# Handing work across the loop boundary of a planned four-layer kernel: the last tail, the first scan operands, the first depthwise operands and a sample's load

## The chip, the cores and the metric

The kernel runs on one core of one Trainium2 chip. The core has five engines, each with its own in-order queue: TensorE (PE), VectorE (DVE), ScalarE (ACT), GpSimd (POOL) and SyncE (SP), which only issues transfers here. The metric is the device time of the whole program in microseconds (us), the median of several runs; lower is better.

## The reference

The input is x of shape (64, 96, 28, 28) in float32. Four layers follow each other, each with a residual.

```python
# layer 0, per sample: a conditional inverted bottleneck, 576 hidden channels, 4 experts
rw  = softmax(relu(mean(x) @ r_w1.T + r_b1) @ r_w2.T + r_b2)      # routing weights
h   = silu(bn1(conv1x1(x, exp_w)))
h   = silu(bn2(dwconv5x5(h, sum_e rw[e] * dw_w[e])))              # per-sample kernels
h   = h * sigmoid(silu(mean(h) @ se_w1.T) @ se_w2.T)              # squeeze and excite
x   = x + bn3(conv1x1(h, sum_e rw[e] * pw_w[e]))
# layers 1 and 3: inverted bottleneck with fixed weights
h   = relu(bn1(conv1x1(x, w1)))
h   = relu(bn2(dwconv3x3(h, wd)))
x   = x + bn3(conv1x1(h, w3))
# layer 2: each sample is cut into four 14 x 14 images; for each image
n   = group_norm(x);  a = silu(conv1x1(n, p1));  u = silu(dwconv3x3(conv1x1(n, p2)))
# selective scan in 4 directions (rows, columns, both reversed), 196 steps, 16 states
h_t = exp(delta_t * A) * h_(t-1) + (delta_t * u_t) * B_t;   y_t = <h_t, C_t> + D * u_t
y   = a * group_norm(sum of the 4 directions)
x   = x + y * sigmoid(relu(mean(y) @ ca_w1.T) @ ca_w2.T)
```

## The kernel before

**Stages.** Samples run through the four layers as a pipeline. `slot` (L1462) issues the work of one step. In the slot of sample t, layer 2 works on sample t (`mamba`, in two halves of two images), layer 1 on t+1, layer 0 on t+2 and layer 3 on t-1; the first expansion of layer 1 for sample t+2 is issued too ("ahead"). At the slot's end the finished sample t-1 is stored (L1477) and sample t+3 is loaded (L1487). Four tiles `xt` hold the samples in flight.

**Blocks.** A block is a stretch of slots that is planned as one. There are nine executions of three blocks: the opening with slot 0, a hardware loop (`For_i`, L1543) with eight slots in its body, run seven times (56 slots), and a last block of seven slots. A plan knows nothing of the block before it or after it; at the jump back to the loop's start all engines meet.

**The planner.** `Plan.op` records an operation with its engine, an estimated cost, what it reads and writes, and a due time. `Plan.run` then places the operations one by one: on each engine those that can start within a grace of each other compete, and the earliest due goes first. The order that results is written down as the order of each engine's queue. The due time is a nominal one, slot number times `T` (144.0) plus a place within the slot, plus a shift from the table `DUE`, which has an entry for each kind of operation (a kind is the function that issues it and the layer it is for). An operation is not started more than 45 us ahead of its due time. Where `run` expects TensorE to idle, it fills the hole with matmuls of zeros (L527).

**Buffers.** Every pool in `POOLS` has a fixed number of buffers, and `run` picks one when it places the operation that first writes it: 3 of `rep` and `wd`, 2 of `B` and `C`, 4 of `dd`, 1 of `y`, 5 PSUM banks `ps`. `take` makes a new tile under the buffer's name.

**Layer 2.** `head` computes the norms, u, a and the scan's inputs, and sends them to DRAM (`bcd`, `ddd`). `scans` (L1254) fetches them spread over lanes with SyncE: B, three dd tiles and C (L1251). ScalarE computes the decays (L1322), VectorE the products b (L1340), then a forward scan h (L1345) and a backward scan g (L1350), 12 pairs for each half; GpSimd adds and multiplies (L1300); TensorE sums over states into y (L1274). `tail` (L1368) takes y, starting with L1377 on VectorE, and does the group norm (L1096 to L1116), the gating (L1407), two small matmuls and the gate (L1429), which writes the sample's half.

**Convolutions.** `expand` issues the 1x1 matmuls (L717, L747), their evictions (L701) and the stores to DRAM `ex` (L734, L760). `load` fetches for a unit of channels the shifted rows `rep` (L772) and the weights `wd` (L801 from DRAM; for layer 0 POOL builds them, L576). `depthwise` runs on TensorE (L819), with evictions on ScalarE (L830). `project` is L888 on TensorE, and L900 adds the residual on VectorE. Layer 0 also has `routing` (L927 to L956, mixing at L916 and L918).

Of the kernel before, what the change touches and what calls it, by code (L numbers as in the profile page):

```python
# [163 lines left out]
def pack_l2(ins):  # L164
# [54 lines left out]
    -11, 24, -20, -15, -10, 25, -7, -25, 9, 6, 16, -2, 2, 11, -18, 5, 31, -17, -8, -16, 22, 1, -6, 26, 19, -9,  # L219
    11, 14, -14, 13, -11, 0, -18, 13, -4, -1, 16, -5, 22, -5, 12, -9, -6, 2, 3, 1, 4, 28, 1, 25, -4, -5, 9,  # L220
    -17, -3, -4, 21, -13, -6, 9, 17, 21, -20, 30, 3, 7, -13, 3, -11, 11, 40, 2, -12, 24, -9, -21, 29, -7, 15,
    14, 13, -10, 9, -1, 8, 4, 15, 8, 24, -22, -9, 11, -21, -8, -4, 16, 4, -12, 7, 8, -17, 33, -3, -13, 8, 24,
    -3, 10, 22, 24, 12,)


class Buf:


    def __init__(self, pool):
        self.pool, self.ap, self.users, self.left, self.end = pool, None, 0, 0, 0.0  # L230
# [9 lines left out]
class Plan:  # L240
# [15 lines left out]
    def __init__(self, kernel):  # L256
        self.k = kernel
        self.ops = []
        self.writer, self.readers, self.latest = {}, {}, {}
        self.due, self.tag = 0.0, None  # L260

    def buf(self, pool):
        return Buf(pool)
# [46 lines left out]
    def run(self, start=0.0):  # L310
        free = dict.fromkeys(GRACE_KEYS, start)
        slots = {name: [None] * n for name, n in self.k.slots.items()}
        queue = {e: [] for e in free}
# [7 lines left out]
        def place(o):  # L321

            t = 0.0
            need = {}
            for b in o.allocs:
                need[b.pool] = need.get(b.pool, 0) + 1
            for pool, n in need.items():
                ends = sorted(0.0 if s is None else s.end for s in slots[pool] if s is None or not s.left)
                if len(ends) < n:
                    return None  # L330
                t = max(t, ends[n - 1])
            return t

        while left:
# [55 lines left out]
            for b in o.allocs:  # L390
                s = slots[b.pool]
                i = min((i for i in range(len(s)) if s[i] is None or not s[i].left), key=lambda i: s[i].end if s[i] else 0.0)
                s[i] = b
                b.ap = self.k.take(b.pool, i)
# [9 lines left out]
            self.emit(o, last)  # L404
        self.span = max(free.values())
# [54 lines left out]
class Kernel:  # L460
    T = 144.0
# [26 lines left out]
    def __init__(self, ctx, tc, x, out, blobs, packs):  # L488
# [12 lines left out]
        for i in range(4):  # L501
            nc.sync.dma_start(self.xt[i], self.x[i])
# [14 lines left out]

        self.b = pool("terms", 1, space=PSUM).tile([P, 1024], F32, name="b")
# [12 lines left out]
    def take(self, pool, i):  # L531
        return self.pools[pool].tile(self.POOLS[pool][1], F32, tag=f"{pool}{i}", name=pool)
# [50 lines left out]
    def setup(self, fold, banks):  # L583
# [91 lines left out]
        self.npad = self.ndecay = 0  # L675

# [99 lines left out]
    def load(self, d, u):  # L776

        nc, pl, k, cb, layer = self.nc, self.plan, d["k"], d["cb"], d["layer"]
        pl.tag = layer
        if layer == 0:  # L780
            ch, n = 64 * u, 4
        else:
            ch, n = P * u, 4 if u < 4 else 2
        rep, wd = pl.buf("rep"), pl.buf("wd")
        pl.op(
            SP, 0.32 * (k + 1), lambda: self.rows(d, rep, ch, n),
            r=[("ex", d["exkey"], ch // P)], w=[rep], nbytes=(k + 1) * cb * n * 1792, land=4.2 if n == 4 and k == 3 else 2.8,
        )
        m = n * k * 2
        lanes = (k + 1) * cb  # L790

        def spread():
            self.spread_taps(
                wd()[:lanes, : m * cb].rearrange("k (n c) -> k n c", c=cb), d["kern"]()[:, 40 * u : 40 * u + 40], d["c"]("mask")
            )

        if layer == 0:
            pl.op(POOL, 1.45, spread, r=[d["kern"]], w=[wd])
        else:
            pl.op(  # L800
                SP, 0.55, lambda: nc.sync.dma_start(wd()[:, : m * cb], self.taps[layer][u][:, : m * cb]),  # L801
                w=[wd], nbytes=P * m * cb * 4,
            )
        d.setdefault("units", {})[u] = rep, wd
# [236 lines left out]
    def convs(self, base, span, jobs, first=None, ahead=None):  # L1041
# [12 lines left out]
        for i, (d, after) in enumerate(jobs):  # L1054
# [6 lines left out]
            for u in range(units):  # L1061
                pl.due = at(u / units) - 14.0
                self.load(d, u)
# [184 lines left out]
    def spread(self, pool, key, due, src):  # L1248
        nc, pl = self.nc, self.plan
        t = pl.buf(pool)  # L1250
        pl.op(SP, 0.58, lambda: nc.sync.dma_start(t(), src), r=[key], w=[t], nbytes=602112 if pool == "dd" else 401408, due=due)  # L1251
        return t

    def scans(self, q, at):  # L1254
# [3 lines left out]
        y = q["y"] = pl.buf("y")  # L1258

        def states(lane, k):  # L1260

            v = self.bcd[i2][lane + 8 * k : lane + 8 * k + 8].rearrange("(a n u) l -> a n (u l)", a=1, u=2)
            return v.to_broadcast([32, 4, 2 * HALF])

        def channels(j):

            v = self.ddd[i2][32 * j : 32 * j + 32].rearrange("c (a l) -> c a l", a=1)
            return v.to_broadcast([32, 4, 3 * HALF])
# [37 lines left out]
        for k in range(2):  # L1306
            B = self.spread("B", ("bcd", i2), at(6 * k) - 14.0, states(0, k))
            if k == 0:
                for j in range(J):
                    dd[j] = self.spread("dd", ("ddd", i2), at(2 * j) - 14.0, channels(j))  # L1310
            Cs = self.spread("C", ("bcd", i2), at(6 * k) - 10.0, states(32, k))
            ys = []
            for j in range(J):
                i = 2 * (J * k + j)
                n = self.ndecay % len(self.decays)
                self.ndecay += 1
                fs = self.decays[n]

                def decay(fs=fs, d=dd[j], k=k, j=j):
                    for u in range(2):  # L1320
                        at = (2 * k + u) * J + j
                        nc.scalar.activation(  # L1322
                            fs[:, :, u, :, :SEQ],
                            d()[:, :2].rearrange("p o (i l) -> p o i l", i=2),
                            AF.Exp,
                            scale=self.A[:, at : at + 1],
                        )

                pl.op(ACT, 1.9, decay, r=[dd[j]], w=[("decay", n)], table=EXP, due=at(i) - 9.0)
# [112 lines left out]
    def mamba(self, t, base, span, more):  # L1442
# [6 lines left out]
        for h, q in enumerate(qs):  # L1449
            self.scans(q, lambda i: at(h * n + i))  # L1450
# [8 lines left out]
            self.tail(q)  # L1459
        yield  # L1460

    def slot(self, i, t, load, store, expanded=True, last=0, lead=0.0):  # L1462
# [5 lines left out]
        m = self.mamba(t, base - lead, span, last < 2)  # L1468
        next(m)
        jobs = []  # L1470
        if last < 2:
            jobs.append((self.job(1, t + 1, 0), None))
# [12 lines left out]
        if load is not None:  # L1485
            pl.due = base + span - 10.0
            pl.op(SP, 0.4, lambda: nc.sync.dma_start(self.xt[(t + 3) % 4], load), w=keys(t + 3), nbytes=301056)  # L1487
        for _ in m:
            pass

# [44 lines left out]
def mk_conv_seq_kernel(ctx, tc, x, out, blobs, packs):  # L1535
# [5 lines left out]
    k.slot(0, 0, None, None, lead=45.0)  # L1541
    pl.run(-150.0)
    with tc.For_i(0, (n - 4) // 8, 1) as it:  # L1543
        pl = k.block()
        for j in range(8):
            k.slot(j, 1 + j, at(k.x, it * 8 + 4 + j), at(k.out, it * 8 + j))
# [3 lines left out]
    for j in range(left):  # L1550
        load = k.x[n - left + 3 + j] if j < left - 3 else None
        k.slot(
            j, 1 + j, load, k.out[n - left - 1 + j], expanded=j < left - 1, last=max(0, j + 3 - left)
# [25 lines left out]
```

## Time and profile before

| what | value |
|---|---|
| median of 3 runs | 10218.62 us (10200.85 to 10236.85) |
| the profiled execution: time | 10215.28 us |
| the profiled execution: span, first to last instruction | 10213.4 us |
| granted TensorE clock, mean | 0.960 of full speed |
| transfers | 2262 MB, 222 GB/s |
| forward and backward scans | 2751.2 and 2726.3 us of VectorE |

The profile is of one execution. "Busy" is the time in which an engine carries out instructions; a wait is put down to what ended last before it was over. Rows of the timeline give start and length in us, engine, line of the kernel, operation, and tiles as out<-in with partitions and elements; a bracket at the end is the idle time before the instruction and what released it. SPq and ACTq are the queues of SyncE and ScalarE as they issue transfers.

### The profile page before, as it was taken

The numbers are of one execution on the slowest core, as the hardware profiler recorded it, in microseconds if no ns is written. First come the engines' busy times: TensorE is split into PE (matmuls) and PEld (weight loads), VectorE is DVE, ScalarE is ACT, GpSimd is POOL, SyncE is SP. The second block draws the span as 40 slices with busy tenths as digits, with TensorE's granted clock in tenths as the row PEclk, the third lists the DMA queues.
The fourth block names the chain that finished last, engine by engine and source line by source line (L and its number), as shares of the span: only waits on it lengthen the run. The fifth ranks groups of instructions, "written<-read, shape, count | busy, mean of one in ns | idle before, by whom it ended". The sixth has DMA issues, their size and how long they took to land. (4 is left out here: it accounts for less than half of the span.)

```text
span 10213.4 us, 198801 instructions
## 1 busy us (share of the span) xinstructions
PE 9466.1 (93%) x76420; PEld 4010.3 (39%) x76420; DVE 8646.1 (85%) x8704; ACT 6558.8 (64%) x10733; POOL 7322.7 (72%) x7517
## 2 busy tenths in 40 slices
PE   7899999999989999999999999999999999999996
PEld 3333343343333443334443434434433344433442
DVE  2788997888978988788887889888897888888897
ACT  3467666667656666566666676666766666766663
POOL 2677776777767777677776777777776777767775
PEclk9999999999999999999999999999999999999998
DMA  7678887888878888788887788788887888878883
GB/s 200 167 214 231 243 233 212 227 226 235 245 195 228 230 233 235 202 228 237 230 223 218 215 240 236 205 227 219 239 239 213 217 235 233 236 217 212 237 241 106
DMA packets 1132623, 2262.48 MB, mean 222 GB/s; under 512 B 105984, under 2 KB 891136, under 8 KB 1131520
## 3 DMA queue, kind: packets, MB, share of 16 engines
q1 hardware_dynamic: 877120, 1750.74, 66.8%
q10 hardware_dynamic: 254528, 498.71, 13.8%
q8 instruction: 616, 10.09, 0.4%
q14 instruction: 359, 2.94, 0.1%
HBM read 1725.52 MB, written 523.50 MB: 220 GB/s over the span
## 5 line engine op out<-in xcount | busy, mean ns | idle before, releaser
L819 PE MATMUL ps<-rep,wd 128*32 128x392 f32 (+1 forms) x50688 | 4729.5, 510 | 318.4 <-DMA rep<-ex 68.9
L1345 DVE TENSOR_TENSOR_SCAN h<-decay,b 128x788 f32<-128x788 f32 x1536 | 2751.2, 1791 | 392.2 <-POOL g L1300 153.1
L819 PEld LDWEIGHTS ps<-rep,wd 128*32 128x32 f32 (+1 forms) x50688 | 1624.8, 110 | 2917.8 <-issue 2293.3
L1350 DVE TENSOR_TENSOR_SCAN g<-decay,b 128x788 f32<-128x788 f32 x1536 | 2726.3, 1775 | 25.8
L1300 POOL TENSOR_TENSOR yc<-h,g 128x392 f32<-128x392 f32 x1536 | 1576.6, 1045 | 1109.5 <-DVE b L1340 647.9
L830 ACT ACTIVATE acc<-ps,l_bn2b,l_bn2s 128x392 f32<-128x392 f32 x1728 | 1157.3, 673 | 1698.3 <-PE ps L819 1397.1
L1300 POOL TENSOR_TENSOR yc<-yc,C 128x392 f32<-128x392 f32 x1536 | 1564.3, 1036 | 416.8 <-DVE b L1340 339.2
L1340 DVE TENSOR_TENSOR b<-dd,B 128x784 f32<-128x784 f32 x1536 | 1812.2, 1180 | 38.5 <-DVE g L1350 0.5
L1322 ACT ACTIVATE decay<-dd,A 128x784 f32<-128x784 f32 x1536 | 1364.3, 942 | 680.3 <-DMA dd<-ddd 413.4
L1300 POOL TENSOR_TENSOR g<-h,g 128x392 f32<-128x392 f32 x1536 | 1568.8, 1041 | 299.6 <-DVE b L1340 277.9
L1300 POOL TENSOR_TENSOR yc<-yc,g 128x392 f32<-128x392 f32 x1536 | 1430.4, 950 | 154.8 <-DVE b L1340 154.8
L717 PE MATMUL ps<-x,blob 96*128 96x392 f32 x3072 | 1285.7, 554 | 111.5 <-PEq L1543 30.5
L701 ACT ACTIVATE border<-ps,l_bn1b,l_bn1s 128x392 f32<-128x392 f32 x1536 | 985.2, 675 | 387.4 <-PE ps L717 262.5
L576 POOL TENSOR_TENSOR wd<-kern,blob 96x640 f32<-96x640 f32 x576 | 767.8, 1340 | 328.0 <-PE ps L819 155.4
L717 PEld LDWEIGHTS ps<-x,blob 96*128 96x128 f32 x3072 | 579.0, 206 | 763.9 <-issue 277.9
L888 PE MATMUL ps<-acc,blob 128*96 128x392 f32 (+1 forms) x2560 | 827.3, 505 | 28.2 <-ACT border L701 13.6
L888 PE MATMUL ps<-acc,wp 128*96 128x392 f32 x2304 | 772.2, 494 | 11.9 <-DVE wp L1028 11.5
L1322 ACT ACT_TABLE_LOAD x422 | 541.4, 1283 | 84.4 <-ACT border L701 37.7
L888 PEld LDWEIGHTS ps<-acc,blob 128*96 128x96 f32 (+1 forms) x2560 | 353.8, 163 | 460.0 <-issue 363.2
L888 PEld LDWEIGHTS ps<-acc,wp 128*96 128x96 f32 x2304 | 372.9, 163 | 406.6 <-issue 372.7
L1274 PE MATMUL y<-yc,blob 128*32 128x392 f32 x3072 | 449.6, 523 | 63.3 <-POOL yc L1300 62.1
L1115 POOL TENSOR_TENSOR gs<-gs,mhalf 96x2 f32<-96x2 f32 x256 | 189.2, 739 | 375.9 <-ACT gs L1112 302.5
(149 smaller groups left out, 7862.6 us busy)
## 6 DMA issues: line engine op xcount, KB each, us to landing
rep<-ex SPq DMA_DIRECT2D x1024, 448.0 KB, 7.7
rep<-ex SPq DMA_DIRECT2D x1984, 224.0 KB, 5.2
ex<-border ACTq DMA_DIRECT2D x512, 480.0 KB, 5.5
dd<-ddd SPq DMA_DIRECT2D x384, 588.0 KB, 6.9
wd<-taps SPq DMA_DIRECT2D x512, 384.0 KB, 7.1
ex<-border ACTq DMA_DIRECT2D x256, 512.0 KB, 6.3
B<-bcd SPq DMA_DIRECT2D x256, 392.0 KB, 4.2
C<-bcd SPq DMA_DIRECT2D x256, 392.0 KB, 5.5
```

What stands on the lines that cost most here:

```text
L576: self.nc.gpsimd.tensor_tensor(out, taps.rearrange("k (n a) -> k n a", a=1).to_broadcast([k, n, cb]), mask.rearrange("k (a c) -> k a c", a ...
L701: nc.scalar.activation(dst, ps()[:, :HALF].rearrange("p (r o w) -> p o r w", o=2, w=28), d["func"], bias=bias[:, t : t + 1], scale=scale[: ...
L717: nc.tensor.matmul(ps()[:, :HALF], w1[:, t * P : t * P + P], x[:, h * HALF : (h + 1) * HALF], start=True, stop=True)
L819: nc.tensor.matmul(ps()[lo : lo + 32, :HALF], w, rep()[: (k + 1) * cb, b, :, 2 - off + dx : 30 - off + dx], start=(dx == 0), stop=(dx == k ...
L830: nc.scalar.activation(acc()[lo : lo + n], ps()[lo : lo + n, :HALF], d["func"], bias=bias[lo : lo + n, at : at + 1], scale=scale[lo : lo + ...
L888: nc.tensor.matmul(banks[o]()[:C, :HALF], w, a, start=(i == 0), stop=(i == (8 if d["layer"] == 0 else 4)))
L1274: nc.tensor.matmul(y()[32 * j : 32 * j + 32, :HALF], c("sel"), ys[j]()[:, 2 * u : 2 * u + 2], start=(k == 0 and u == 0), stop=(k == 1 and ...
L1300: nc.gpsimd.tensor_tensor(*vs, op)
L1322: nc.scalar.activation(fs[:, :, u, :, :SEQ], d()[:, :2].rearrange("p o (i l) -> p o i l", i=2), AF.Exp, scale=self.A[:, at : at + 1],)
L1340: nc.vector.tensor_tensor(out, v, w, ALU.mult)
L1345: lambda h=h, ff=ff: nc.vector.tensor_tensor_scan(flat(h()), ff, b, 0.0, ALU.mult, ALU.add),
L1350: lambda g=g, ff=ff: nc.vector.tensor_tensor_scan(flat(g())[:, ::-1], ff[:, ::-1], b[:, ::-1], 0.0, ALU.mult, ALU.add),
```

## The change

The plans stay separate, but what one block has begun can be taken up by the next. A buffer can now be tied to a numbered place (`slot` in `Buf`). `sent` buffers are remembered in `carry` at the end of a plan; `carried` ones occupy their place from the start of the next plan, and their reader needs no load. So that the same memory is meant on both sides, the tiles of `rep`, `wd`, `B`, `dd` and `y` are made once (`fixed`).

The last slot of the opening block and of the loop body is called with `on=True`. It

- leaves out the tail of its second half, and pins `y` to place 0 for it;
- loads `rep` and `wd` of unit 0 of the next layer-1 job, due 14 us ahead of the slot's end;
- loads B and the first two dd tiles of the next sample's first half (due 14, 14 and 11 us ahead of the end), and computes the first decay (due 8 us ahead);
- in the loop, does not load a sample.

The first slot of the loop body and of the last block takes these up: it runs the handed-over tail first (due at the block's start), skips the loads and the decay that are there, and fetches the sample t+2 that the slot before did not load (`late`, due 25 us ahead of the start). The opening loads three samples and not four. `T` goes from 144.0 to 142.0, and the table `DUE` has other numbers, and 112 entries where it had 111; new operations give new kinds.

```diff
 DUE = (
-    -11, 24, -20, -15, -10, 25, -7, -25, 9, 6, 16, -2, 2, 11, -18, 5, 31, -17, -8, -16, 22, 1, -6, 26, 19, -9,
+    -15, 34, -30, -1, 8, 36, -7, -40, 19, 30, 11, 28, 4, 15, -12, 5, 29, -40, -20, 11, 13, 11, 0, 20, 13, -11,
...
+    def carried(self, pool, slot):
+
+        b = Buf(pool, slot, self.k.carry[pool, slot])
+        self.taken.append(b)
+        return b
...
     def run(self, start=0.0):
         free = dict.fromkeys(GRACE_KEYS, start)
         slots = {name: [None] * n for name, n in self.k.slots.items()}
+        for b in self.taken:
+            slots[b.pool][b.slot] = b
...
             for b in o.allocs:
+                if b.slot is not None:
+                    s = slots[b.pool][b.slot]
+                    if s is not None:
+                        if s.left:
+                            return None
+                        t = max(t, s.end)
+                    continue
...
+        for b in self.sent:
+            self.k.carry[b.pool, b.slot] = b.ap
...
-    T = 144.0
+    T = 142.0
...
-        for i in range(4):
+        for i in range(3):
             nc.sync.dma_start(self.xt[i], self.x[i])
...
+        self.fixed = {
+            (name, i): self.pools[name].tile(self.POOLS[name][1], F32, tag=f"{name}{i}", name=name)
+            for name in ("rep", "wd", "B", "dd", "y") for i in range(self.POOLS[name][0])
+        }
...
-                self.load(d, u)
+                if u not in d.get("units", ()):
+                    self.load(d, u)
...
+    def ahead(self, q, due):
+
+        pl, i2 = self.plan, q["i"]
+        pl.tag = None
+        B = self.spread("B", ("bcd", i2), due - 14.0, self.states(i2, 0, 0), 0)
+        dd = [self.spread("dd", ("ddd", i2), due - 14.0 + 3.0 * j, self.channels(i2, j), j) for j in range(2)]
+        return dict(B=0, dd=(0, 1), decays=[self.decay(dd[0], 0, 0, due - 8.0)])
...
-            self.scans(q, lambda i: at(h * n + i))
+            self.scans(q, lambda i: at(h * n + i), begun if h == 0 else None, on and h == 1)
...
-            self.tail(q)
+            if not (on and h == 1):
+                self.tail(q)
         yield
...
+        begun, self.begun = self.begun, None
+
+        def fetch(src, t, due):
+            pl.due = due
+            pl.op(SP, 0.4, lambda: nc.sync.dma_start(self.xt[t % 4], src), w=keys(t), nbytes=301056)
+
+        if late is not None:
+            fetch(late, t + 2, base - 25.0)
+        if begun:
+            q = self.half(t - 1, 1)
+            q["y"] = pl.carried("y", 0)
+            pl.due = base
+            self.tail(q)
+        m = self.mamba(t, base - lead, span, last < 2, begun, on)
         next(m)
         jobs = []
         if last < 2:
-            jobs.append((self.job(1, t + 1, 0), None))
+            d = self.job(1, t + 1, 0)
+            if begun:
+                d["units"] = {0: (pl.carried("rep", 0), pl.carried("wd", 0))}
+            jobs.append((d, None))
...
         if load is not None:
-            pl.due = base + span - 10.0
-            pl.op(SP, 0.4, lambda: nc.sync.dma_start(self.xt[(t + 3) % 4], load), w=keys(t + 3), nbytes=301056)
+            fetch(load, t + 3, base + span - 10.0)
         for _ in m:
             pass
+        if on:
+            pl.due = base + span - 14.0
+            self.load(ahead, 0, 0)
+            self.begun = self.ahead(self.half(t + 1, 0), base + span)
...
-    k.slot(0, 0, None, None, lead=45.0)
+    k.slot(0, 0, None, None, lead=45.0, on=True)
...
-            k.slot(j, 1 + j, at(k.x, it * 8 + 4 + j), at(k.out, it * 8 + j))
+            k.slot(
+                j, 1 + j, at(k.x, it * 8 + 4 + j) if j < 7 else None, at(k.out, it * 8 + j), on=j == 7,
+                late=None if j else at(k.x, it * 8 + 3),
+            )
...
-            j, 1 + j, load, k.out[n - left - 1 + j], expanded=j < left - 1, last=max(0, j + 3 - left)
+            j, 1 + j, load, k.out[n - left - 1 + j], expanded=j < left - 1, last=max(0, j + 3 - left),
+            late=None if j else k.x[n - left + 2],
```

`self.decay`, `self.states` and `self.channels` are the functions that stood inside `scans`, moved out of it unchanged.

## The prediction

> **What bounds the kernel now.** I read the page first, then the times between scans, then a table of windows by slot, then the timeline across one end of a loop block, then SyncE's waits and the transfers there. The page's busy times:
>
> ```profile
> PE 9466.1 (93%) x76420; PEld 4010.3 (39%) x76420; DVE 8646.1 (85%) x8704; ACT 6558.8 (64%) x10733; POOL 7322.7 (72%) x7517
> ```
>
> TensorE and VectorE are both nearly full, so the time is set by their order, not by one of them. VectorE's scans give the clock hand: a sample has 24 forward scans (L1345) and 24 backward ones (L1350). Listing them in order of time and taking, for each sample, the end of its last backward scan (called E below) to the start of the next sample's first forward scan, I get 1.25 us on average inside a block, but 39.5 us (37.2 to 41.9) at the six jumps back to the loop's start, 74.4 us at the entry into the loop and 35.2 us at its exit. The spacing of samples by position in the block, mean of seven blocks, is 145.7, 158.5, 153.3, 152.5, 148.3, 148.8, 149.3 and 185.5 us, together 1241.9. Positions 4 to 6 show the settled slot, 148.8. Eight such are 1190.4, so a block loses 51.5: 37.6 in the gap (mean of jumps and exit, less 1.25), 17.9 in positions 1 to 3, and -4.0 in position 0 and the scans of position 7. Windows by slot of one block (columns: length; busy us and instructions of PE, its weight loads, DVE, ACT, POOL; granted clock, DMA share, GB/s), first, second, seventh and last slot:
>
> ```profile
> 1670.70:1815.70 145.00, 135.45 (x1094) 56.50 (x1093) 129.65 (x116) 91.94 (x143) 107.72 (x111) 0.93 0.82 221
> 1815.70:1974.80 159.10, 144.99 (x1204) 61.95 (x1203) 135.40 (x137) 102.47 (x168) 117.83 (x119) 0.95 0.82 220
> 2578.70:2726.50 147.80, 141.02 (x1187) 59.63 (x1186) 133.94 (x137) 102.17 (x169) 113.00 (x118) 1.00 0.87 239
> 2726.50:2909.70 183.20, 169.28 (x1280) 72.25 (x1280) 139.29 (x157) 115.69 (x194) 118.35 (x124) 0.97 0.75 208
> ```
>
> The last slot has 44 us without VectorE work, the seventh 14. The timeline across that end (start, length, engine, line, operation), E = 2870.4:
>
> ```profile
> 2868.62 1.78 DVE L1350 TENSOR_TENSOR_SCAN g<-decay,b 128x788 f32<-128x788 f32 x1
> 2876.66 1.52 PE L1274 MATMUL y<-yc,blob 128*32 128x392 f32 x12
> 2878.26 0.62 DVE L1377 SCALAR_TENSOR_TENSOR u<-u,D,y 96x392 f32<-96x392 f32 x1 [7.86 <-PE y L1274]
> 2884.79 0.90 PE L888 MATMUL ps<-acc,blob 64*96 64x392 f32 x4
> 2885.72 1.16 DVE L900 SCALAR_TENSOR_TENSOR x<-ps,l_bn3b,x 96x392 f32<-96x392 f32 x2 [5.77 <-PE ps L888]
> 2886.91 0.37 SPq L1477 DMA_DIRECT2D out_dram<-x  x1
> 2889.52 0.37 SPq L1487 DMA_DIRECT2D x<-x_dram  x1
> 2891.11 0.75 DVE L1429 SCALAR_TENSOR_TENSOR x<-ps,cz,x 96x196 f32<-96x196 f32 x2 [2.48 <-ACT cz L1423]
> 2894.85 0.56 SPq L1251 DMA_DIRECT2D B<-bcd  x1
> 2895.05 5.28 PE L717 MATMUL ps<-x,blob 96*128 96x392 f32 x8 [5.08 <-PEq L1543]
> 2895.47 0.59 SPq L1251 DMA_DIRECT2D dd<-ddd  x1
> 2905.16 0.17 DVE L945 TENSOR_TENSOR ps<-ps,blob 128x4 f32<-128x4 f32 x1 [8.40 <-PE ps L940]
> 2905.57 1.79 ACT L1322 ACTIVATE decay<-dd,A 128x784 f32<-128x784 f32 x2
> 2905.70 0.97 DVE L1340 TENSOR_TENSOR b<-dd,B 128x784 f32<-128x784 f32 x1
> 2907.98 1.78 DVE L1345 TENSOR_TENSOR_SCAN h<-decay,b 128x788 f32<-128x788 f32 x1
> ```
>
> Five stretches are to be seen: 7.9 us until y is collected, 13.6 us of tail (L1377 to L1429, 2878.3 to 2891.9), 3.0 us until the next block's first instruction, 10.9 us until its first product, 2.3 until its first scan. But TensorE's last projection also ends late, at E+15.3, and its residual add at E+16.5; these are not the tail's. SyncE's wait at the loop's end, and the two transfers there (KB, us to landing):
>
> ```profile
> SPq L1543 <- DMA x<-x_dram: 3.2, 1, 3.2
> ```
>
> ```profile
> out_dram<-x SPq DMA_DIRECT2D x1, 294.0 KB, 2.6
> x<-x_dram SPq DMA_DIRECT2D x1, 294.0 KB, 3.8
> ```
>
> So the jump waits until transfers in flight have landed: x at 2893.3, the first instruction 1.5 us later.
>
> **The skill beside it.** "DMA: Bandwidth & Descriptors", section "Rules for kernel authors", says to issue a transfer early, compute, and wait for it late. The trace bears it out here: B landed 3.5 us after issue, the dd issues of this start took 8.6, and only then could the decay at 2905.57 run. Handing them over is that rule applied across a jump; but the trace adds that the jump itself is a wait for every transfer, so the gain exists only if they land before E+19. "TensorE: Matmul & The Clock Gate", "What's actually happening", says that an idle window of about 3.4 us halves the clock and a busy one restores it. In the trace, the clock records show half speed for 17 to 27 us out of the first 30 after each of the six jumps, and eight L717 matmuls took 5.28 us (0.66 each) against 0.35 each at 2868.85, the loop end's own twelve in 4.19. I go by these durations: a shorter hole gives back a few us of clock, not the whole of positions 1 to 3.
>
> **The change, part by part** (profiled execution: span 10213.4, time 10215.28, that is 3.3 below the median 10218.62).
>
> *Tail of the last half moved into the next block.* Takes E+7.9 to E+21.5 off the block's end. What is late next is the projection: last add ends E+16.5, the store is issued there and lands 2.6 later, E+19.1; with the 1.5 us from landing to first instruction the next block begins at E+21 instead of E+24.4. Only 3.4 of 13.6 are won. Moved in are 3.5 us of VectorE (0.62, statistics 1.05, gating about 1.0, gate 0.83), and some 3 us of ScalarE, between scans. It holds y (one buffer), but the next collect is 20 us off; and u and a of half 1, which the next head rewrites, as everywhere inside a block.
>
> *B, two dd tiles, the first decay handed over.* The first product can start at once: 10.9 us become 0 to 1.7 (if the tail's first two VectorE operations go ahead), the decay no longer precedes the scan. First scan at E+22.3 to E+24; I take 23.5 against 39.5: -16.0. But statistics of the head, routing and tail (3.5+3.2 us of VectorE), which lie in the hole now, fall between scans again; position 0 goes from 145.7 to the settled 148.8, +3.1. The three loads, 1568 KB, go ahead of the jump, where the windows show DMA at 0.35 of its time (2878.2 to 2894.8). The decay's 1.79 us and perhaps one more table load (1.283 us on the page) are hidden behind TensorE's last 7 us; without that cover they would cost up to 3.1 a jump.
>
> *rep and wd of unit 0 handed over.* TensorE's first depthwise (L819) came at 2914.31, 43.9 after E, now at about E+22. rep needs the ex store issued at 2871.15, landing 5.5 (page) to 9.4 (here): E+6 to E+10; rep itself 7.7: E+14 to E+18. It just fits before E+19.1; each us late is a us lost. With it the positions after the jump should start less behind. Of their 17.9 I count 4 (bounds 0 and 17.9), for the half-speed stretch alone costs 8 x 0.31 = 2.5.
>
> *x load moved from the last slot to the next block's start* (for sample t+2). It leaves the jump's wait (3.8, already counted) and stands first in SyncE's queue: 0.37 us for C, rep, wd behind it. Routing (L927) waits about 4 us for it; its product kern is first read by POOL at 2946.3, kern was done at 2917.4, so 29 us of slack: nothing. Ends of queues (POOL's turn, fixed tile names in place of a new tile per use): the same waits by data, nothing; the opening loads one sample fewer, 3.8 us in a stretch hidden by weights.
>
> *Due shifts and T.* They reorder all five queues. The trace has no row for the new order. Bounds: TensorE's matmuls without the zero-filling ones take 138.6 us in a settled slot, so at best -10; position 1, the same work in another phase, is +9.7. I take 0, with 2 us a slot either way (settled slots vary from 146.3 to 150.2 but for one of 154.3).
>
> **Sum.** Six jumps: 16.0 - 3.1 + 4 = 17, together 102. Exit (35.2 to 23.5): 11.7 - 3.1 + 4 = 13. Entry: nothing waits for all engines there; VectorE's last add ends at E+47, so the scan could start at E+50 instead of 74, less 3 for position 0: 21; but TensorE's depthwise, at 441.1, gains only to about 428 (ex store 412.85, +7.5, +7.7): 13. I take 17. Total 132: 10215.28 - 132 = 10083, with the 3.3 to the median about **10085**.
>
> **Rivals.**
> 1. *More* (0.27): the reordering also lets TensorE's projection end with the scans. Then the jump hangs on y, E+8, gap about 12.5, 27 a boundary, 216; with 1 us less in 56 settled slots: 9945. For it: the projection lagging 15 us is an order, not a need. Against: TensorE is the fuller engine.
> 2. *Little* (0.18): handed-over loads hold the jump; rep lands at E+24, scan at E+28: 39.5-28-3.1 = 8 a boundary, 64: 10150. For it: the 1 to 5 us margin above; 14 us landings when five loads start together at the present block start. Against: idle DMA before the jump.
> 3. *Slower* (0.15): the new order makes the settled slot longer, at positions 3 to 6, where an in-order queue (ScalarE's between TensorE's banks and the decays) puts an eviction behind a waiting decay. At +4 us a slot, 64 slots cost 256, less 132: 10340. It decides from 2.1 us a slot (132/63). For it: position 1 against 5. Against: nothing in a settled slot's data flow is changed.
> 4. *Not as said*: handed-over tiles might be waited for anew; that is rival 2's time.
>
> **Chances.** Forecast 0.40, rivals 0.27, 0.18, 0.15. About 0.3% (31 us) is what a measurement can tell from no change. Faster: nearly all of the first two and three quarters of rival 2, 0.77; within 0.3% 0.08; slower 0.15. The range reaches to 9900 (rival 1 with a better order) and up to 10235, leaving out the slower case; the likeliest case alone, with 12 to 22 a jump, is 10045 to 10125.
>
> **What would show it.** Gap at jumps near 23 us, tail rows after the jump, first L819 within 3 us of it, no SyncE wait for x but one for the store; settled slots at 148.8 plus or minus 2. Wrong if the settled slots move by over 2 us, or if SyncE's wait names rep or dd.

## The result: 1.7% slower, and the profile after

| | before | after |
|---|---|---|
| median, same session (4 runs each) | 10217.81 us (10200.85 to 10236.85) | 10394.91 us (10379.7 to 10407.64) |
| ratio, 95% interval | 1 | 1.0172 [1.0148, 1.0196] |
| profiled execution: span | 10213.4 us | 10401.4 us |
| granted TensorE clock, mean | 0.960 | 0.938 |

10085 was forecast, and at most 10235; it became 10395. The page of after has less matmul work than before (75888 instructions against 76420; the difference is zero-filling, 356 instructions where before has 888) in a longer span:

```profile
PE 9431.4 (91%) x75888; PEld 3950.9 (38%) x75888; DVE 8580.1 (82%) x8704; ACT 6576.3 (63%) x10755; POOL 7429.4 (71%) x7517
```

**The joint between blocks came out as forecast.** This is the timeline across the same end of a loop block as before (start, length, engine, line, operation, in brackets the idle time before it). E, the end of the last backward scan, is 2930.60:

```profile
2928.82 1.78 DVE L1407 TENSOR_TENSOR_SCAN g<-decay,b 128x788 f32<-128x788 f32 x1
2938.38 1.26 SPq L804 DMA_DIRECT2D rep<-ex  x2
2939.28 1.52 PE L1335 MATMUL y<-yc,blob 128*32 128x392 f32 x12
2947.90 1.16 DVE L932 SCALAR_TENSOR_TENSOR x<-ps,l_bn3b,x 96x392 f32<-96x392 f32 x2 [17.30 <-PE ps L920]
2949.09 0.36 SPq L1554 DMA_DIRECT2D out_dram<-x  x1
2953.09 0.98 DVE L1397 TENSOR_TENSOR b<-dd,B 128x784 f32<-128x784 f32 x1 [4.03 <-PEq L1623]
2953.17 0.37 SPq L1533 DMA_DIRECT2D x<-x_dram  x1
2953.29 4.15 PE L851 MATMUL ps<-rep,wd 128*32 128x392 f32 x24 [5.42 <-PEq L1623]
2954.93 1.76 DVE L1402 TENSOR_TENSOR_SCAN h<-decay,b 128x788 f32<-128x788 f32 x1
2956.61 0.59 DVE L1434 SCALAR_TENSOR_TENSOR u<-u,D,y 96x392 f32<-96x392 f32 x1
```

and this SyncE's wait at the loop's end (us in total, times, longest):

```profile
SPq L1623 <- DMA out_dram<-x: 10.2, 7, 1.8
```

No tail row (L1434) stands ahead of the jump; the product b is VectorE's first instruction after it, TensorE starts with its depthwise (L851), and the only transfer that the jump waits for is the store. As the prediction put it, the last residual add (L932) now ends last. It ends at E+18.5, and the first scan starts at E+24.3.

**The slots between the joints did not.** Windows by slot, the same four of the same block as before, cut at each sample's first backward scan (length; busy us and instructions of PE, its weight loads, DVE, ACT, POOL; granted clock, DMA share, GB/s):

```profile
1698.36:1849.12 150.76, 134.00 (x1091) 55.91 (x1094) 133.64 (x129) 102.93 (x168) 114.50 (x116) 0.93 0.77 213
1849.12:2001.20 152.08, 146.29 (x1206) 61.42 (x1202) 133.99 (x137) 99.14 (x165) 114.84 (x118) 0.97 0.82 231
2623.71:2779.98 156.27, 143.06 (x1182) 60.00 (x1176) 132.92 (x137) 102.24 (x168) 115.63 (x117) 0.95 0.82 225
2779.98:2958.19 178.21, 160.89 (x1288) 67.58 (x1280) 135.24 (x143) 109.34 (x175) 118.46 (x120) 0.94 0.76 211
```

The seventh slot, settled, took 147.80 us before at clock 1.00, and now takes 156.27 at 0.95 with the same work. The mean of seven blocks, by position in the block, from first backward scan to first backward scan, with the time in which the clock records show half speed (they hold nothing but full and half speed):

| position | 0 | 1 | 2 | 3 | 4 | 5 | 6 | 7 | sum |
|---|---|---|---|---|---|---|---|---|---|
| before, us | 145.7 | 158.5 | 153.3 | 152.5 | 148.3 | 148.8 | 149.3 | 185.5 | 1241.9 |
| after, us | 152.6 | 152.7 | 157.5 | 156.6 | 157.0 | 156.1 | 156.2 | 179.6 | 1268.4 |
| at half clock, before | 17.8 | 16.6 | 13.2 | 13.2 | 3.4 | 1.5 | 3.4 | 15.8 | 84.8 |
| at half clock, after | 22.5 | 9.8 | 19.0 | 17.6 | 17.1 | 16.6 | 17.1 | 23.7 | 143.3 |

The account of the two spans (+188.0): up to sample 1's first scan -24.1; in the loop +185.5, of which the seven gaps give -103.0 and the slots +288.5; last block and end +26.5. So the expected gain was won and more than twice as much lost, all over the program, in slots whose data flow the hand-over does not touch. A settled slot (positions 4 to 6) went from 148.8 to 156.4.

**What the settled slot waits for.** The timeline of one of after, around the mixing of the layer-0 expert weights:

```profile
2417.20 1.03 SPq L833 DMA_DIRECT2D wd<-taps  x2
2418.28 1.44 SPq L804 DMA_DIRECT2D rep<-ex  x2
2419.83 0.55 SPq L833 DMA_DIRECT2D wd<-taps  x1
2420.42 1.23 SPq L804 DMA_DIRECT2D rep<-ex  x2
2421.22 0.66 ACT L948 ACTIVATE ps<-expert,rw 128x480 f32<-128x480 f32 x1
2421.91 14.43 SPq L1027 DMA_DIRECT2D expert<-w  x4
2424.90 1.46 DVE L950 SCALAR_TENSOR_TENSOR ps<-expert,rw,ps 128x480 f32<-128x480 f32 x2
2427.26 2.16 PE L1042 MATMUL ps<-sc,blob 24*128 24x1 f32 x18
2435.27 0.72 DVE L950 SCALAR_TENSOR_TENSOR ps<-expert,rw,ps 128x480 f32<-128x480 f32 x1 [6.59 <-DMA expert<-w]
2435.90 0.16 DVE L1046 TENSOR_TENSOR sc<-ps,blob 128x9 f32<-128x9 f32 x1
2436.10 0.21 ACT L1050 ACTIVATE sc<-sc 128x9 f32<-128x9 f32 x1 [7.80 <-DVE sc L1046]
2436.12 1.54 PE L1240 MATMUL ps<-u,blob 96*48 96x392 f32 x2 [3.71 <-DVE sc L1046]
2437.10 1.02 POOL L1361 TENSOR_TENSOR yc<-yc,C 128x392 f32<-128x392 f32 x1 [7.17 <-DVE b L1397]
```

and the same place in before:

```profile
2382.19 0.33 SPq L801 DMA_DIRECT2D wd<-taps  x1
2382.56 1.23 SPq L772 DMA_DIRECT2D rep<-ex  x2
2386.19 9.64 SPq L995 DMA_DIRECT2D expert<-w  x4
2388.03 1.46 DVE L918 SCALAR_TENSOR_TENSOR ps<-expert,rw,ps 128x480 f32<-128x480 f32 x2
2391.17 0.17 DVE L1014 TENSOR_TENSOR sc<-ps,blob 128x9 f32<-128x9 f32 x1
2391.62 0.20 ACT L1018 ACTIVATE sc<-sc 128x9 f32<-128x9 f32 x1
2394.76 0.72 DVE L918 SCALAR_TENSOR_TENSOR ps<-expert,rw,ps 128x480 f32<-128x480 f32 x1 [2.46 <-DMA expert<-w]
2395.70 0.86 PE L1207 MATMUL ps<-u,blob 96*48 96x392 f32 x2
```

In both, the last mixing of the first half waits for that half's fourth expert load, the first of SyncE's row of four. There are three expert buffers for four loads: three loads went out some 90 to 120 us earlier, and the fourth is issued only when ScalarE's first mixing (L948) has set its buffer free (it ends at 2421.88). In this slot of before it landed about 8.5 us after its issue, with three transfers of rep and wd issued ahead of it and still in flight; in this slot of after, with seven, about 13.3. Seven is the most that is seen: over the 21 settled slots the load for which VectorE waits longest met 4.2 transfers in flight (1810 KB) and landed after 8.3 us in before, and met 6.4 (2706 KB) and landed after 12.5 us in after. And in before VectorE had the add of the excitation (L1014) ahead of that wait; in after the add (L1046) is queued behind it. It takes 0.16 us, but ScalarE's gate, a PSUM bank for TensorE's small matmul L1240 and GpSimd's next product all hang on VectorE there. In the list of waits of after (engine, line, waited for: us in total, times, longest):

```profile
ACT sc L1050 <- DVE sc L1046: 349.4, 55, 8.4
DVE ps L950 <- DMA expert<-w: 304.1, 67, 6.8
PE ps L1240 <- DVE sc L1046: 172.3, 53, 5.7
```

Before, the second of them was

```profile
DVE ps L918 <- DMA expert<-w: 169.6, 74, 4.6
```

and the other two were 7.4 us (9 times) and 31.0 us (8 times). In after, the rows of ScalarE and TensorE come 55 and 53 times in 64 samples: from position 1 of each block on, the same waits come back from slot to slot. That order is the candidate. The experiments ask first whether it is the table or the hand-over that makes it, and then what in it costs the time.

### The profile page after: what moved, and what is told of

Read it like the earlier page. It is cut to its first block, busy times and chain, and to the rows that moved or that the text cites. A ratio compares the mean times of both kernels' runs of the same rounds, so it can differ in the third digit from the quotient of the medians.

```text
span 10401.4 us, 197683 instructions
## 1 busy us (share of the span) xinstructions
PE 9431.4 (91%) x75888; PEld 3950.9 (38%) x75888; DVE 8580.1 (82%) x8704; ACT 6576.3 (63%) x10755; POOL 7429.4 (71%) x7517
## 5 line engine op out<-in xcount | busy, mean ns | idle before, releaser
L851 PE MATMUL ps<-rep,wd 128*32 128x392 f32 (+1 forms) x50688 | 4940.3, 531 | 394.2 <-ACT acc L862 83.6
L851 PEld LDWEIGHTS ps<-rep,wd 128*32 128x32 f32 (+1 forms) x50688 | 1685.2, 113 | 3174.1 <-issue 2548.9
L1361 POOL TENSOR_TENSOR yc<-yc,C 128x392 f32<-128x392 f32 x1536 | 1633.4, 1079 | 655.1 <-DVE b L1397 603.3
L1397 DVE TENSOR_TENSOR b<-dd,B 128x784 f32<-128x784 f32 x1536 | 1750.4, 1140 | 76.3 <-PEq L1623 24.2
L1361 POOL TENSOR_TENSOR yc<-yc,g 128x392 f32<-128x392 f32 x1536 | 1461.0, 971 | 103.3 <-DVE b L1397 103.3
L749 PE MATMUL ps<-x,blob 96*128 96x392 f32 x3072 | 1173.4, 517 | 108.3 <-ACT acc L862 75.2
L749 PEld LDWEIGHTS ps<-x,blob 96*128 96x128 f32 x3072 | 544.9, 191 | 675.7 <-issue 192.3
L950 DVE SCALAR_TENSOR_TENSOR ps<-expert,rw,ps 128x480 f32<-128x480 f32 (+1 forms) x384 | 254.1, 662 | 367.1 <-DMA expert<-w 304.1
L932 DVE SCALAR_TENSOR_TENSOR x<-ps,l_bn3b,x 96x392 f32<-96x392 f32 x384 | 226.8, 617 | 388.2 <-PE ps L920 388.1
```

The lines of the kernel that those rows point to most:

```text
L749: nc.tensor.matmul(ps()[:, :HALF], w1[:, t * P : t * P + P], x[:, h * HALF : (h + 1) * HALF], start=True, stop=True)
L851: nc.tensor.matmul(ps()[lo : lo + 32, :HALF], w, rep()[: (k + 1) * cb, b, :, 2 - off + dx : 30 - off + dx], start=(dx == 0), stop=(dx == k ...
L950: nc.vector.scalar_tensor_tensor(out if e == E - 1 else acc, src, rw[:, e : e + 1], acc, ALU.mult, ALU.add)
L1361: nc.gpsimd.tensor_tensor(*vs, op)
L1397: nc.vector.tensor_tensor(out, v, w, ALU.mult)
```

## The experiments

Before ran beside each group, at 10216 to 10224 us. Spacings, gaps and half-clock times are worked out from each trace as above; "settled" is the mean of positions 4 to 6. The expectations call TensorE's L1240 the xp matmul.

**1. The hand-over under the old table.** All shifts as before, T = 144; the late load alone keeps its shift of -5, for the old table has none (the expectation's "shift of 0" is a slip).

```diff
-DUE = (-15, 34, -30, -1, 8, 36, ...)   # after
+DUE = (-11, 24, -20, -15, -10, 25, ...)   # before, at the new numbers
-    T = 142.0
+    T = 144.0
```

> All of the hand-over, with the shifts and the nominal slot (144) of the kernel before; the one new kind of operation, the late load, keeps its shift of 0. Theory A (the table lengthens the settled slot, the hand-over does what was forecast): settled slot 148 to 150 us, gap at the jumps 23 to 26 us, time 10060 to 10140, ratio 0.985 to 0.993. Theory B (the hand-over itself, its fixed tiles and pinned places, lengthens the slots): settled slot 154 to 157 and 10350 to 10400.

Measured: 10271.35 us, ratio 1.0048 [1.003, 1.0066]. The gaps are short (22.3 at the jumps, 47.1 at the entry, 21.7 at the exit), and still it is slower than before: positions 0 to 7 take 149.1, 164.7, 150.6, 156.3, 149.3, 156.4, 155.9, 167.9, sum 1250.2. Only position 4 comes near the settled 148.8 of before, though not a shift was changed: other operations at a block's start are enough for another order in its later slots. Neither theory has it: the gaps are short, as in A, and positions 3, 5 and 6 as long as in B. Yet these long slots are not after's. ScalarE's wait for the add is 19.3 us in the whole run, and VectorE waits 2.3 us a settled slot for expert loads.

**2. The new table without the hand-over.** Before, with the new shifts and T = 142.

```diff
-DUE = (-11, 24, -20, -15, -10, 25, ...)
+DUE = (-15, 34, -30, -1, 8, 36, ...)   # at the old numbers
-    T = 144.0
+    T = 142.0
```

> The kernel before with the new shifts (that of the late load left out) and the nominal slot of 142; nothing is handed over. Theory A: settled slot 155 to 158 us, gap at the jumps about 38, time 10500 to 10600. Theory B: settled slot 148 to 150, time 10200 to 10240.

Measured: 10533.2 us, ratio 1.0304 [1.0286, 1.0322]; gaps 43.4, 78.1 and 40.4; positions 1 to 6 at 155.2 to 161.6. Its waits are after's, at before's lines:

```profile
ACT sc L1019 <- DVE sc L1015: 330.2, 48, 8.8
DVE ps L919 <- DMA expert<-w: 326.0, 64, 7.5
PE ps L1208 <- DVE sc L1015: 151.9, 46, 5.6
```

So the long order of after comes with the new table and T, without any hand-over; that the hand-over alone leads to long slots of another kind was seen in 1. The four corners (10395 is from the result's runs, where before had 10218):

| | old table, T = 144 | new table, T = 142 |
|---|---|---|
| no hand-over | 10222 | 10533 (+311) |
| hand-over | 10271 (+49) | 10395 (+173) |

Under the new table the hand-over is worth 138 us, under the old one it costs 49: the two do not add.

**3. T alone.** After with T = 144.

```diff
-    T = 142.0
+    T = 144.0
```

> The changed kernel with the nominal slot of 144 in place of 142, shifts unchanged. If the shifts do it: settled slot 155 to 158, time 10360 to 10430. If the shorter nominal slot does it: settled slot near 149, time near 10100.

Measured: 10282.91 us, 1.007 [1.0046, 1.0093], 112 less than after. Positions 1 and 2 take 148.3 and 149.4; then the plan falls into the long order, 157.1, 155.2 and 156.1 at positions 4 to 6. The new table allows both; which is taken hangs on what came before.

**4. Eight shifts.** After, with the shifts of the squeeze, the expert loads, the mixing and the excitation (kinds 18 to 25) as before.

```diff
-    ..., -20, 11, 13, 11, 0, 20, 13, -11, ...
+    ..., -8, -16, 22, 1, -6, 26, 19, -9, ...
```

> The changed kernel with the old shifts for the eight kinds of squeeze-and-excite and the expert loads alone (18 to 25). If the late expert transfers, for which VectorE waits 5.7 us a slot (before: 3.2), are the main cost: VectorE's wait for them falls to about 3 and the slot by 2.5 to 5 us, time 10080 to 10240. If the loss is spread over many kinds: under 1 us a slot, time over 10330.

Measured over 12 runs: 10211.44 us, 0.9987 [0.9977, 0.9996] against before, and 183 less than after. Eight of 112 numbers take back what after lost against before, though not what the hand-over was to bring. Settled 148.6 (150.7, 147.6, 147.4). VectorE stands for 5.2 us ahead of the mixings of a settled slot, nearly as long as in after (5.7), but for another cause: 2.2 us of it are for expert loads, as the expectation had it, and the rest for ScalarE's first mixing, which itself waits little for loads (28.7 us in the whole run). For the whole run:

```profile
DVE ps L951 <- ACT ps L949: 182.8, 79, 27.9
DVE ps L951 <- DMA expert<-w: 177.5, 112, 5.4
```

The load for which VectorE waits longest lands 7.6 us after its issue here, against 12.5 in after. Other waits of VectorE are gone too (tail's L1434 0.4 instead of 4.0, the residual add 0.3 instead of 2.9, the gating 0 instead of 2.8); kernel 5 below, which has them and a slot of 150.1, shows that they cost little. The gap at the jumps is 31.4 here, and position 0 takes 157.7.

**5 and 6. No wait for experts, in both kernels.** The plan is kept and the loads are issued, but the mixing reads a constant tile.

```diff
-                src = lambda t=t, n=n: t()[:, : n * C].rearrange("p (g o) -> p g o", g=n)
+                src = lambda t=t, n=n: c.tiles[0][:, : n * C].rearrange("p (g o) -> p g o", g=n)
```

> The changed kernel, every queue in its order, its expert loads still issued and moved, but layer 0's mixing of the projection weights reads a constant tile in place of the loaded experts, so nobody waits for these loads (the projection's weights are not the reference's). Theory C (the late expert loads start a chain: VectorE in order, the PSUM banks it holds, TensorE, SyncE's own queue): settled slot 156.4 falls by 5 to 8 us, half-speed time from 17 to under 8, TensorE's wait at its xp matmul from 3.2 to under 0.5, time 9950 to 10100. Theory D (the loss is spread over the new order, each wait its own): the slot falls by the 2.5 us by which this wait exceeds that of before, time 10220 to 10290.

> The same cut in the kernel before, as a control: VectorE waits 3.2 us a settled slot there for these loads. Theory C: settled slot 148.8 falls by 2 to 3 us, 10040 to 10110. If this wait costs nothing in itself in the kernel before (something else is as late): under 1 us, over 10160.

Measured: in after 10068.97 us (0.9854 [0.9831, 0.9877] of before, 326 less than after), settled 150.1; in before 10148.22 (0.9929 [0.9906, 0.9951], 75 less), settled 148.6. In the order of after the waits for experts carry 6.3 of the 7.6 us, with VectorE's waits at the tail (2.9), the residual add (2.2) and the gating (2.8) still there. What hung on them goes as well; ScalarE's wait for the add, 349.4 us in after, is

```profile
ACT sc L1050 <- DVE sc L1046: 82.3, 55, 2.4
```

In before, 3.0 us of waiting for these loads in a settled slot carry 0.2. But its position 1, where that wait is 6.5 us, falls by 6.5 (158.5 to 152.0), and most of the 75 us come from positions 0 to 2. So a short wait was free there and a long one was not; whether its length or the order around it decides is not separated. The cut takes away two things together, VectorE's wait for the landing and SyncE's wait for a free expert buffer.

**7. Another group of shifts.** After, with the tail's shifts (kinds 73 to 87) as before.

```diff
-    ..., 23, -3, -36, 39, -2, 10, 14, 19, -36, 35, 4, -11, 3, 27, -15, ...
+    ..., 24, -9, -21, 29, -7, 15, 14, 13, -10, 9, -1, 8, 4, 15, 8, ...
```

> The changed kernel with the old shifts for the fifteen kinds of the tail alone (73 to 87), as a control to the squeeze-and-excite group. If the settled order is fragile (any group put back moves the plan into another order that repeats): settled slot off 156.4 by over 3 us, time under 10330. If squeeze-and-excite is what matters: 155 to 158, 10370 to 10420.

Measured: 10353.18 us, 1.0134 [1.0114, 1.0154]; settled 153.1. Some of it comes back, from a third order. So the tail's shifts count for less than the eight of 4; that no other group of eight would do as much is not shown by this one control.

**8. Experiments 3 and 4 together.** After, with the eight old shifts and T = 144.

```diff
-    ..., -20, 11, 13, 11, 0, 20, 13, -11, ...
+    ..., -8, -16, 22, 1, -6, 26, 19, -9, ...
-    T = 142.0
+    T = 144.0
```

> The changed kernel with the old squeeze-and-excite shifts and the nominal slot of 144. Each alone gained (10211 and 10283). If the gains add: 10100. If both only move the plan to another order that repeats: anything from 10150 to 10400, with a gap at the jumps of 24 to 32.

Measured over 14 runs: 10182.98 us, 0.996 [0.9948, 0.9972]. It beats both kernels, by 0.4 and 2.0%: gap 28.2 at the jumps, 28.1 at the exit, positions 156.9, 148.3, 150.1, 148.1, 156.7, 149.2, 149.9, 178.8. Its wait for the expert loads is no smaller than before's:

```profile
DVE ps L951 <- DMA expert<-w: 196.0, 109, 6.9
```

but ScalarE's for the add, 349.4 us in after, is 4.3. Still, it is only 41 us below before, where the hand-over alone was to bring 132: some of the gap is given back, and positions 0 and 4 are 7 to 8 us above the others.

**9. The add ahead of the wait.** After with its plan, but in VectorE's queue the add L1046 changes places with the mixing that waits.

```diff
+            if o.mark == "add":
+                self.emit(o, last)
+                self.flush(last)
...
+        elif o.mark == "mix":
+            self.held = o
```

> The changed kernel with one pair of neighbours exchanged in VectorE's queue in each slot: the excitation's add (L1046), which frees a PSUM bank and lets ScalarE compute the gate, goes ahead of the mix that waits for the fourth expert load; all other queues keep their order. C1 (the 0.2 us add caught behind the waiting mix is what carries the wait to TensorE and ScalarE): TensorE's wait at the xp matmul from 3.2 to under 1 us a slot, slot 3 to 5 us shorter, 10090 to 10220. C2 (VectorE's own stall, or SyncE's queue held by the expert buffers, carries it): slot less than 1.5 us shorter, over 10300.

Measured: 10323.3 us, 1.0101 [1.0074, 1.0128], 72 less than after; settled 154.8, only 1.6 less. The waits behind the add go as meant (this kernel's L1074 and L1253 are after's L1050 and L1229):

```profile
ACT sc L1074 <- DVE sc L1070: 56.0, 55, 2.2
PE ps L1253 <- ACT acc L884: 171.7, 54, 5.5
```

The first was 349.4 us, but the second, 8.0 us in after, is new. TensorE's 3.2 us before the matmul L1240 of a settled slot are gone, as C1 had it, and its wait before the next small matmul (L1229) rises from 2.6 to 4.95: 2.4 of the 3.2 passed on, and the time is nearly C2's. They passed on by way of ScalarE: with its gate done early it comes sooner to its own mixing of the second half (L970), which needs the next expert load, and its accumulators stand behind that. This wait was 0.7 us in after:

```profile
ACT ps L970 <- DMA expert<-w: 225.6, 53, 5.8
```

**10. One mixing without its wait.** As in 5, for the last mixing of the first half alone.

```diff
-                src = lambda t=t, n=n: t()[:, : n * C].rearrange("p (g o) -> p g o", g=n)
+                src = lambda t=t, n=n, k=e == 3 and lo == 0: (c.tiles[0] if k else t())[:, : n * C].rearrange("p (g o) -> p g o", g=n)
```

> The changed kernel, all orders kept, with only the fourth mix of the first half reading a constant tile, so that one of the eight expert loads of a slot is not waited for (the projection's weights are not the reference's). If that one wait carries the loss: nearly all of what cutting all eight gave (326 us), 10070 to 10150. If the other seven have a part: half of it or less, 10200 to 10330.

Measured: 10310.11 us, 1.0094 [1.0065, 1.0122]; settled 154.2, 2.2 less than after. TensorE before L1240: 0; before L1229: 4.6 us, with 153.5 us for ScalarE's accumulator in the list of waits. It is ScalarE again that now waits for the next load:

```profile
ACT ps L948 <- DMA expert<-w: 197.6, 53, 5.1
```

So even the longest wait, taken away, is worth a third of what all the mixings' waits are worth together (6.3); the later loads of the row still come late.

**11 and 12. Telling the planner the landing.** The plan's estimate of an expert load's time to landing set to 9.0 us (it reckoned some 2 us and the bytes), in after and in kernel 8.

```diff
-                    w=[t], nbytes=P * n * C * 4, due=due - 15.0,
+                    w=[t], nbytes=P * n * C * 4, due=due - 15.0, land=9.0,
```

> The changed kernel with one number of its planner set to what was measured: an expert load is taken to land 9 us after its issue. The table and the nominal slot of 142 stay; the plan orders itself anew. If the loss comes from the plan not knowing of this lateness: VectorE's expert wait falls from 5.7 to under 3 us, slot 148 to 152, 10080 to 10250. If the table's order is bad in itself: slot over 154, over 10330.

> The same number in the version with the old squeeze-and-excite shifts and the nominal slot of 144 (10183 before this edit), where the expert wait is 5 us a slot. If the lateness still costs there: 10050 to 10130. If that order hides it, as in the kernel before: 10150 to 10220.

Measured: 11084.54 us (1.0843 [1.0813, 1.0872]) and 10604.63 (1.038 [1.0355, 1.0405]). The estimate is nearer to the trace, and the plans are far worse: 151 to 174 us at positions 1 to 6 of the first, and a gap of 52.8 us at its jumps. In kernel 12 the wait in question has nearly gone,

```profile
DVE ps L951 <- DMA expert<-w: 21.6, 29, 1.8
```

with 196.0 us in kernel 8, and the slots are longer by up to 16 us at positions 2, 4 and 6. The shifts were not remade for the new estimate, so this says nothing against a true estimate with its own table. It says that removing this wait is no aim by itself.

Not tried: SyncE's hold for an expert buffer apart from VectorE's wait (with a fourth buffer, say), and the half clock apart from the waits (TensorE's holes would have to be filled, and the zero-filling needs a bank free at that moment).

## Why the prediction was wrong

**Right.**
- *The joint.* Gap 23.5 forecast at jumps and exit, 24.3 and 23.3 measured; about E+50 at the entry, 49.0. First L851 at E+22.7, forecast about E+22. rep, issued at 2938.38, has landed by E+15 (forecast E+14 to E+18), so rival 2, the jump held by handed-over loads, is out. The jump waits for the store alone, and the late sample load costs nothing to be seen.
- *Part of the joint by luck.* The prediction took the 10.9 us from the first instruction to the first product as waiting for loads, with 8.6 us for dd. That is the median of two loads: the first dd tile, the one needed, was issued at 2895.47 and landed 4.8 us later, at 2900.3, and B before it. The product ran at 2905.70 because VectorE's queue had routing's add (L945) ahead of it, which waited 8.4 us for TensorE. So about half of the 10.9 us was order. In after the product stands first in the queue, and both parts went together.
- *The skill's rule on loads* (DMA: Bandwidth & Descriptors, Rules for kernel authors), to issue early and wait late, held at the joint: b and the first depthwise start at once. The settled slot shows what happens without it: with three buffers for four experts the fourth load is issued late, at 2421.91, behind others, and the wait for it has an in-order queue behind it.
- *The sum of the hand-over, 132 us*: from kernel 2 to after it is 138. The agreement is largely luck. The gaps gave more than forecast there (19.1 us at each jump, from 43.4, and 29.1 at the entry), and the slots gave some back. Under the old table, for which the sum was made, the same hand-over costs 49.

**Wrong.** The failed step is "Due shifts and T", and in it the sentence "I take 0, with 2 us a slot either way". Measured alone (kernel 2) the reordering costs 311 us, with settled slots 9.6 us longer; in after they are 7.6 longer. The bounds beside it, -10 and +9.7, held; the value between them was a choice, and the range that followed from 2 us a slot was too narrow. Rival 3 had the mechanism (the settled slot longer by the new order, deciding from 2.1 us a slot), with +4 us for 10340 and a chance of 0.15; its place was another. It named an eviction in ScalarE's queue behind a waiting decay; the runs showed VectorE's mixing waiting for an expert load, with an add of 0.16 us behind it in the queue. "Against: nothing in a settled slot's data flow is changed" was true and no argument: the data flow left room for slots of 148 and of 174 us. The sum also took the order as one thing and the hand-over as another; kernel 1 shows that the hand-over by itself changes the order of later slots.

**Where the 7.6 us of a settled slot go.** TensorE's busy time without the zero-filling (useful), the filling, its idle time and VectorE's wait for expert loads alone, us per settled slot:

| | spacing | useful | filling | idle | at half clock | wait for experts |
|---|---|---|---|---|---|---|
| before | 148.8 | 139.9 | 2.3 | 6.6 | 2.8 | 3.0 |
| after | 156.4 | 144.1 | 0 | 12.3 | 16.9 | 5.7 |
| 5, no wait for experts | 150.1 | 141.6 | 0 | 8.5 | 10.4 | 0 |
| 9, add ahead | 154.8 | 143.4 | 0 | 11.4 | 14.6 | 4.7 |
| 4, eight old shifts | 148.6 | 140.1 | 1.8 | 6.7 | 8.0 | 2.2 |

In after TensorE idles 5.7 us more: it stands 3.2 before L1240 and 2.6 before L1229, where it did not stand before, 0.8 more before L749, and about 1 us less elsewhere. It also needs 4.2 us more for the same matmuls, with 14 us more of half clock in the slot; and 2.3 us of filling are gone. Together 7.6. The idle time before L1240 and, in part, L1229 is shown to hang on the waits for experts (5, 9 and 10). That the half clock follows from the holes is argued from their falling together in kernel 5, not shown by itself.

**Shown, and not.** Shown: after's order comes with the new table and T (2), and either the eight shifts around the mixing (4) or T (3) put back takes 183 or 112 us off; in that order the waits for experts, with SyncE's hold, carry 6.3 of 7.6 us (5); no single wait carries it, for ScalarE then waits for the next load (9, 10); with 2.2 us of waiting for loads the settled slot is 148.6 again (4). A short wait for loads is not enough: kernels 1 and 12 have it, and long slots by other waits. Not shown: whether a wait as long as after's could be free in another order. Open: why the hand-over under the old table ends 49 us above before. Its gaps save 144 us (six jumps 17.2 each, entry 27.3, exit 13.5), and orders of 150 to 165 us at positions 1 to 6 take it back; which operation tips the plan out of its settled order was not isolated.

**Smaller misses.** Position 0 was to rise to a settled 148.8 and rose to 152.6. The stretch after the jump was to have a few us less at half clock, and has 22.5 us against 17.8, though TensorE starts at once. Of the 17.9 us by which positions 1 to 3 stood above settled ones, 4 were to go; in after they stand 2.5 below three settled slots of the new order.

## What to carry to other kernels

When a change comes with a new schedule, cost the two apart, and do not put the schedule at 0: with the data flow unchanged it was the larger term here, and a range must take in the bounds that the trace gives for it. A wait in an in-order queue is not priced by its own length: 3.0 us a slot for these loads cost 0.2 us in one order, and 5.7 us cost 6.3 in another, where it was longer and more hung on it. Split the idle time ahead of an instruction by what ended it, before it is laid on a load. Where a planner is greedy, a piece of work moved at a block's start changes each slot after it, so measure the change with the old table and with the new.

## What the runs showed of the hardware

- Landing time grew with what was in flight at the issue, on SyncE's and ScalarE's queues together. In settled slots of before, a load of some 226 KB met 1810 KB in flight and landed after 8.3 us; in after, one of 240 KB met 2706 KB and landed after 12.5. Both come to some 240 to 250 GB/s for what was in flight and the load itself.
- The half clock came after quite short holes. In settled slots of kernel 4 no hole of TensorE is longer than 2.2 us, in 5 none longer than 2.9, and the clock records still show half speed for 8.0 and 10.4 us a slot, nearly always in stretches of 3.4 or 6.8 us. In after (half of the holes over 1.4 us, the longest 5.7, TensorE busy for 92%) it was 16.9 us a slot, in stretches up to 13.7. In before, with half of the holes under 0.5 us, the longest 3.1 and 2.3 us of zero-filling, it was 2.8. The skill (TensorE: Matmul & The Clock Gate, What's actually happening) speaks of an idle window of about 3.4 us; the length of the stretches agrees with it, while nearly all holes here are shorter.
